# The last second layers of a perceiver kernel get tighter schedules, and the very last one stands alone behind the loop

## The chip, the cores and the metric

The kernel runs on one core of one Trainium2 chip. The metric is the device time of one execution in microseconds. Below, PE is TensorE (matmuls; PEld are its weight loads), DVE is VectorE, ACT is ScalarE, POOL is GpSimd and SP is SyncE, which issues the transfers.

## The reference

Input `x` has 32 batches of 64 rows of 256 numbers; `ctx_1024` has 32 batches of 1601 rows of 256 numbers. Six blocks are added to `x` one after the other:

```
x = x + xattn0(layernorm(x), ctx)     # a linear layer over x and the mean of ctx
x = x + attn0(layernorm(x))           # 16 heads over the 64 rows, with ALiBi slopes
x = x + ffn0(layernorm(x))            # shared experts, and 8 routed experts (top 2)
x = x + xattn1(layernorm(x), ctx)     # 16 heads: 64 queries against 1601 context rows
x = x + attn1(layernorm(x))           # recurrent block, below
x = x + ffn1(layernorm(x))            # two layers with ternary weights and 8-bit activations

attn1(x):  x = causal_conv(rmsnorm(x)) + x          # width 4 in time, then 256 x 256
           h, g = rmsnorm(x) by 4 heads -> 96 + 96   # a gated linear recurrence over 64 rows
           x = gru_out + x
           x = (silu(n @ w_gate) * (n @ w_value)) @ w_ff_out + x     # n = rmsnorm(x)
ffn1(x):   h = gelu(quant(x) @ ternary(w1).T);  out = quant(h) @ ternary(w2).T
```

## The kernel before

**Tiles and pieces.** The 32 batches are worked on in 16 tiles of two batches, 128 rows. A tile has a *position* 0 to 15 in the order of work; the last position holds tile 0. Almost all of the work is `xattn1`. It is a loop over 208 *pieces*, `g` = 0 to 207, 13 to a position: twelve pieces of 512 context rows for half the heads of one batch, and, as number 9 of each position, a *rest piece* with the last 65 context rows of both batches. The loop is written as a software pipeline with a fixed order on PE, DVE, ACT and POOL. In the turn of piece `g` it issues, in this order:

- `column_scores(g)`: the matmuls `s` (L842, L845, L851), and on ACT the two exponentials `pt` (L857), 1 us each
- `values(g + 4)`: the matmuls `vps` (L236), and on DVE the copy `vau` (L787)
- now and then a small transpose `tpm` (L826) for the row maxima
- **place 0**: steps of the other layers that begin with ACT work
- `row_scores(g + 5)`: the matmuls `r` (L803), and on DVE two maxima over them, `mx` (L810); after every third piece of a half also five small operations on the maxima (L816 to L821)
- place 0.5: steps that need the column form of matmuls
- `weighted(g)`: 64 matmuls `o` (L875), which need `pt` and `vau`
- `keys(g + 6)`: the matmuls `kps` (L248), and on ACT the copy `kt` (L770)
- **place 1**: all other steps

So towards the end of the loop the keys run out after the turn of piece 201, the row scores after that of 202 and the values after that of 203.

**Steps of the other layers.** Everything else (the first layers of later positions, the queries, the expert choice, the second layers) is written as Python generators. Each `yield` ends a *step*, and its value says to which place the next step belongs. An object of `Steps` lays the steps of one generator into the pieces: with `n` steps to do between the times `t0` and `t1` (given in sixteenths of a position and turned into pieces by `planned`), `run` does a step when `done * (t1 - t0) <= (now - t0) * n`. With `place` 3, at most one step is done in each place of a piece, and only if its kind belongs there.

**The second layer** of a position is `recurrent` and `bit_ffn` (L952 to L1133): 30 steps from `x4`, the result of `xattn1`, to the store of the output. What they do, with the names that the profile shows (K: in place 0, the others in place 1):

| steps | work |
|---|---|
| 1, 2 | statistics `st_e`, `mv_e`, `rstd_e` (POOL), `xn_e`, `yb` |
| 3 K, 4, 5 K | `xs_e` (squares on ACT, `rn_e` on POOL, product on DVE), transposes `tp_e`, ACT copies `ypad` |
| 6, 7 | the convolution `cT`: four DVE operations each (L970, L973) |
| 8 | matmuls `pw`, sum `y` |
| 9 K, 10 | `xs_f` |
| 11 K, 12 K | transposes `tp_f`, ACT copies `nT`; matmuls `hg`, four ACT tanh (`gg`, `zz`), DVE `rr` |
| 13, 14 | the gate chain (POOL `zz`; DVE `gg`, `gg`, `gg`, `zz`, a memset and the scan into `rr`, L1014 to L1022) |
| 15 | matmuls `gru`, sum `y`, POOL `xy` |
| 16 K, 17 | `xs_g` |
| 18 K, 19 K | `tp_g`, `nT`; first half of the matmuls `ff`, tanh `fth`, DVE `fm` (L257, L258) |
| 20, 21 K, 22 | `fm` (L260); second half of `ff`; `fm` (L260) |
| 23 | matmuls `ffo`, sum `x` (L1054), statistics `st_h`, `mv_h` |
| 24 | `xn_h`, its largest value `am_h`, scaled and rounded `qt`; POOL `q_h` |
| 25 K, 26 K | transposes `tpq_h`, ACT copy `qT_h`; matmuls `h` (L236) and ACT Gelu (L1124) |
| 27, 28 | `am_i`; two passes over `h` (L1070, L1071), POOL `q_i` |
| 29 K | transposes `tpq_i`, ACT copy `qT_i` |
| 30 | matmuls `h` (L244, L248), `x` (L1132), store to `out` by SP (L1133) |

`x4` of a position is made in the second piece of the next one (`projected`, `wo`). In the loop's place 1 the 128 x 128 matmuls are issued in four column parts (`mmq`, L248); outside it they are whole (L244). Position 15 uses a variant with two halves, `halved`, in place of steps 27 to 29. Tiles of a second layer have mostly one or two buffers per name, so two second layers share them in turn.

**Where the second layers lie before.** That of position p runs from piece 13(p + 1) + 2 over about 20 pieces, so two overlap for some pieces. Position 12: pieces 171 to 191. Position 13: 184 to 204. Position 14: it starts at 197, and 15 of its 30 steps are done when the loop ends. Behind the loop `projected` makes `x4` of position 15, and then the last lines

```
        while plan:
            for s in list(plan):
                s.step()
                ...
```

take one step of position 14 and one of position 15 in turn until both are done. This stretch is called the *tail*.

Of the kernel before, what the change touches and what calls it, by code (L numbers as in the profile page):

```python
# [21 lines left out]
NT = NB * S // P  # L22
# [22 lines left out]
def perceiver_kernel(ctx: ExitStack, tc: tile.TileContext, a: dict, out: bass.AP):  # L45
# [16 lines left out]
    ACT = "ACT"  # L62

    COL = "COL"
# [7 lines left out]
    def mm_tile(shape, name, dtype=F32):  # L72
        return ps_mm.tile(shape, dtype, tag="mm", name=name)
# [176 lines left out]
    def mmq2(o, lhsT, rhs):  # L250
        for c in range(2):
            mmq(o, lhsT(c), rhs(c), c == 0, c == 1)
# [559 lines left out]
    def maxima(h):  # L812

        hf = halves[h]
        ng = small.tile([P, 4], F32, tag="ng", name=f"ng_{hf.name}")
        nc.vector.tensor_reduce(ng, wholes[hf.pos].mx[:, :, h % 4, :], AX.X, ALU.max, negate=True)  # L816
        m = mxp[h % 2]
        nc.vector.tensor_copy(m[:, :, 0], ng)
        nc.vector.tensor_tensor(ng, ng, m[:, :, 0], ALU.subtract)
        nc.vector.tensor_copy(m[:, :, 1], ng)  # L820
        nc.vector.tensor_tensor(m[:, :, 2], ng, m[:, :, 1], ALU.subtract)  # L821

    def maxima_rows(h):
        hf = halves[h]
        t = mm_tile([P, P], f"tpm_{hf.name}", BF16)
        nc.tensor.transpose(t, mxp[h % 2].rearrange("p i c -> p (i c)"), identb)  # L826
        hf.neg = work.tile([P, P], BF16, tag="neg", name=f"neg_{hf.name}", bufs=5)
        nc.vector.tensor_copy(hf.neg, t)
# [113 lines left out]
    def projected(pos):  # L942

        w = wholes[pos]
        o = mm_tile([P, D], f"wo1_{w.ti}")
        mmq2(o, lambda c: w.oT[:, c].rearrange("p b s -> p (b s)"), lambda c: w_o2[:, c, :])
        x = work.tile([P, D], F32, tag="x4", name=f"x4_{w.ti}", bufs=1)
        nc.vector.tensor_tensor(x, o, residues[pos], ALU.add)
        return x
# [185 lines left out]
    def tail(ti, x):  # L1135
        x = yield from recurrent(ti, x)
        yield from bit_ffn(ti, x)
# [107 lines left out]
    class Steps:  # L1245
# [8 lines left out]
        def step(self):  # L1254
            if self.gen is not None:
                self.done += 1
                try:
                    self.kind = next(self.gen)
                except StopIteration:
                    self.gen = None  # L1260

        def run(self, t, place):
            at = place if self.place == 2 and place != 0.5 else self.place
            if self.place == 3:
                if {ACT: 0, COL: 0.5}.get(self.kind, 1) != place:
                    return
                at = place
            if at == place:
                now = t + (0.5 * place if self.place >= 2 else 0)
                while self.gen is not None and self.done * (self.t1 - self.t0) <= (now - self.t0) * self.n:  # L1270
                    self.step()
                    if self.place == 3:
                        break

        def all(self):
# [12 lines left out]
    def first_layer(pos, k=0):  # L1288
        x3[pos] = yield from layer0(order[pos], csums.get(pos), k)

    def queried(pos):
        yield from query(pos, x3[pos])

    def second_layer(pos):
        yield from tail(order[pos], x4[pos])
# [4 lines left out]
    def first():  # L1300

        csum = sums_tile(order[0])
        steps = layer0(order[0], csum, 0, True)
        for _ in range(3):
            next(steps)
            yield
        junk = big.tile([P, L], F32, tag="part", name="junk", bufs=2)
        summed(order[0], csum, 0, 0, ctxs[0][:, 0, :], junk)
        nc.vector.tensor_reduce(csum[:, 1, 0:1], ctxs[0][:, 1, :], AX.X, ALU.add)
        yield  # L1310
        next(steps)
        yield

        n = L // 2
        more = small.tile([P, 1], F32, tag="ss", name="more", bufs=4)
        summed(order[0], csum, 1, 0, ctxs[1][:, 0, :], junk)
        nc.scalar.activation(junk[:, :n], ctxs[1][:, 1, :n], AF.Copy, accum_out=more)
        nc.vector.tensor_reduce(csum[:, 1, 1:2], ctxs[1][:, 1, n:], AX.X, ALU.add)
        nc.vector.tensor_tensor(csum[:, 1, 1:2], csum[:, 1, 1:2], more, ALU.add)
        csums[0] = csum  # L1320
        yield
        x3[0] = yield from steps
        yield from query(0, x3[0])
# [7 lines left out]
    def early_sums():  # L1331
        for pos in range(1, 4):
            yield from sums(pos, 2)
# [3 lines left out]
    def planned(gen, t0, t1, n, place):  # L1337
        plan.append(Steps(gen, t0 * NU / 16, t1 * NU / 16, n, place))

    plan = []  # L1340
    planned(first_layer(2), 2, 15, 26, 2)
    for pos in range(1, NT):
        if pos > 2:
            t0 = 14 * (pos - 3) + 2 + 4 * (pos == 3)
            planned(first_layer(pos), t0, t0 + 27 - 4 * (pos == 3), 28, 3)
        if pos < NT - 1:
            planned(queried(pos), 16 * (pos - 1) + (1 if pos > 1 else 5), 16 * (pos - 1) + 8.5, 6, 0)
        planned(second_layer(pos - 1), 16 * pos + 1.5, 16 * pos + 31, 33, 3)
    for group, t0, t1 in ((range(4, 6), 5.5, 15), (range(6, 9), 16, 42), (range(9, 13), 45, 84), (range(13, 16), 88, 140)):
        planned(sums_of(group), t0, t1, 12 * len(group) + 2, 0)  # L1350
    for c, t0 in ((1, 72), (2, 128), (3, 184)):
# [7 lines left out]
    with tc.manual_schedule(engines={ET.PE, ET.DVE, ET.Activation, ET.Pool}):  # L1359
        ahead, beside, summing = Steps(first()), Steps(first_layer(1, 1)), Steps(early_sums())  # L1360

        def besides():
            if 1 in csums:
                beside.step()

        def scored():
            row_scores(scores.pop(0))

        scores = list(range(5))
        do = {"a": ahead.step, "b": besides, "s": summing.step, "r": scored, "w": late_weights, "m": lambda: maxima(0),  # L1370
              "t": lambda: maxima_rows(0)}
        do |= {f"k{g}": lambda g=g: keys(g) for g in range(6)} | {f"v{g}": lambda g=g: values(g) for g in range(3)}

        for what in """a a a a k1 a a k2 a a s s k3 k0 a a a a s s s s a k4 a v0 v1 a a a s s s s s s b a b a b a b a s w
                    a s s a a a b a a s s s r b r b s s s r k5 b r m s s s r v2 t""".split():
            do[what]()
        if beside.gen is not None:
            plan.insert(0, Steps(beside.gen, 0, 4, 28 - beside.done, 2))
        planned(biased(), 3, 5, 2, 1)
        if summing.gen is not None:  # L1380
            plan.insert(0, Steps(summing.gen, 0, 4.5, 37 - summing.done, 0))
        planned(all_ternary(), 5, 23, 24, 2)

        def run(t, place):
            for s in [s for s in plan if s.t0 <= t]:
                s.run(t, place)
                if t >= s.t1 and t < NU * NT - 1:
                    s.all()
                if s.gen is None:
                    plan.remove(s)  # L1390

        for g in range(NU * NT):
            pos, p = divmod(g, NU)
            if pos + 1 < NT:
                if p == 0:
                    wholes[pos + 1].rest = load_rest(order[pos + 1])
                if p in (2, 9):
                    load_batch(2 * pos + 2 + p // 8)
            column_scores(g)
            if g == 0:  # L1400
                values(3)
            if g + 4 < NU * NT:
                values(g + 4)
            if p == 1 and pos:
                normalise(pos - 1)
            if g == NU * NT - 2:
                normalise(pos, 3)
            if g + 4 < NU * NT and scanned(g + 4)[2] == NP - 1:
                maxima_rows(scanned(g + 4)[1])
            run(g, 0)  # L1410
            if g + 5 < NU * NT:
                row_scores(g + 5)
                if scanned(g + 5)[2] == NP - 1:
                    maxima(scanned(g + 5)[1])
            run(g, 0.5)
            weighted(g)
            if p == NU - 1 and pos < NT - 1:
                gathered(pos)
            if p == 3 * NP and pos == NT - 1:
                gathered(pos, 3)  # L1420
            if g == NU * NT - 5:
                picked()
            in_columns[0] = True
            if g + 6 < NU * NT:
                keys(g + 6)
            if p == 1 and pos:
                x4[pos - 1] = projected(pos - 1)
            run(g, 1)
            in_columns[0] = False
        normalise_last(NT - 1)  # L1430
        x4[NT - 1] = projected(NT - 1)
        plan.append(Steps(second_layer(NT - 1)))
        while plan:
            for s in list(plan):
                s.step()
                if s.gen is None:
                    plan.remove(s)
# [46 lines left out]
```

## Time and profile before

| | |
|---|---|
| median of three runs (lowest, highest) | 2059.86 us (2058.57, 2060.37) |
| the profiled execution, its own time | 2059.22 us |
| its span, first to last instruction | 2057.5 us |
| mean granted clock of TensorE | 0.982 |
| PE, DVE, ACT, POOL busy | 1960.1, 1300.4, 903.7, 324.8 us |
| the chain that ended last | PE 87%, DVE 7%, ACT 2% |
| `s` of pieces 201 to 207 starts in the chain of waits at | 1942.83, 1950.02, 1957.60 (its second half), 1963.13, 1970.33, 1975.13, 1979.43 us |
| last `o` ends, tail begins | 1983.73 us |

A row of the timeline gives the start in us from the span's beginning, the length in us, the engine, the line, the operation, output and inputs, the shapes and how many instructions were merged; in brackets stands the idle time of the engine before it and what ended it. The chain of waits is followed back from the last instruction and names at each time the work that everything after it waited for.

### The profile page before, as it was taken

The page shows a single profiled execution, that of the slowest core. Times are in us where ns is not written, and L with a number is a line of the kernel's source. Part 1 is how long each engine was busy: PE and PEld are TensorE (multiplying, and loading weights), DVE is VectorE, ACT ScalarE, POOL GpSimd, SP SyncE. Part 2 cuts the span into 40 slices and gives each one's busy share as a digit, 9 for nine tenths or more (in the row PEclk, how much of TensorE's full clock was granted, in tenths as well). Part 3 has the DMA queues.
Part 4 walks back from the last instruction along what each step waited for, and adds up shares of the span by engine and source line. Part 5 has one row for each costly group of instructions (what it writes and reads, how often), then busy time and mean ns, then how long its engine had stood idle before and what let it go on. Part 6 is the DMA issues. An engine that isn't in the chain of part 4 may idle for free.

```text
span 2057.5 us, 79682 instructions
## 1 busy us (share of the span) xinstructions
PE 1960.1 (95%) x36771; PEld 1367.5 (66%) x36771; DVE 1300.4 (63%) x2618; ACT 903.7 (44%) x1402; POOL 324.8 (16%) x543
## 2 busy tenths in 40 slices
PE   5889999999999999999999999999999999999975
PEld 3566677667676766676766676766766666666653
DVE  4556766666666765666667666666667766665654
ACT  4345454454545444444545434343443434334331
POOL 2121111111111111111111111111110111000011
PEclk9899999999999999999999999999999999999996
DMA  9225323221222212112120111111011211101000
GB/s 310 105 90 173 122 85 111 79 89 42 93 90 88 95 36 66 59 58 77 61 76 10 50 40 37 49 40 45 6 58 46 68 45 37 58 2 47 3 12 5
DMA packets 54806, 136.90 MB, mean 67 GB/s; under 512 B 13318, under 2 KB 35016, under 8 KB 54472
## 3 DMA queue, kind: packets, MB, share of 16 engines
q1 hardware_dynamic: 53912, 130.99, 18.8%
q8 instruction: 288, 4.72, 1.0%
q10 hardware_dynamic: 560, 0.81, 0.1%
q14 instruction: 46, 0.38, 0.1%
HBM read 125.53 MB, written 6.25 MB: 64 GB/s over the span
## 4 chain that ended last, share of the span: by engine, by line
PE 87%; DVE 7%; ACT 2%; issue 2%; DMA 1%; POOL 1%; SPq 0%; DVEq 0%; ACTq 0%; POOLq 0%
PE vps L236 18%; PE kps L248 15%; PE r L803 11%; PE o L875 9%; PE s L851 9%; PE ff L236 4%; PE s L845 3%; DVE mx L810 2%; PE ffo L248 2%; PE q L236 1%; ACT pt L857 1%; PE wo L248 1%; PE hg L1004 1%; PE k L236 1%; PE sv L236 1%
## 5 line engine op out<-in xcount | busy, mean ns | idle before, releaser
L857 ACT ACTIVATE pt<-s 128x1024 f32<-128x1024 f32 (+1 forms) x416 | 403.1, 1021 | 265.7 <-PE s L851 265.5
L810 DVE TENSOR_REDUCE mx<-r 128x2 f32<-128x1024 f32 x384 | 451.9, 1219 | 97.4 <-PE r L803 97.2
L236 PE MATMUL vps<-w_L_xattn_WvT,ctxT 128*128 128x128 f32 x3072 | 393.4, 281 | 0.0
L770 ACT ACTIVATE kt<-kps,chv 128x512 f32<-128x512 f32 x192 | 132.0, 687 | 584.9 <-PE kps L248 567.7
L236 PEld LDWEIGHTS vps<-w_L_xattn_WvT,ctxT 128*128 128x128 f32 x3072 | 357.4, 191 | 24.7 <-issue 3.4
L248 PE MATMUL kps<-ctxT,w_L_xattn_WkT 128*32 128x512 f32 x2992 | 356.7, 594 | 0.0
L787 DVE COPY vau<-vps 128x512 f32<-128x512 f32 (+1 forms) x208 | 143.5, 690 | 322.1 <-PE vps L236 320.8
L875 PEld LDWEIGHTS o<-pt,vau 128*32 128x32 f32 (+1 forms) x13312 | 197.7, 110 | 132.2 <-issue 118.5
L875 PE MATMUL o<-pt,vau 128*32 128x64 f32 (+1 forms) x13312 | 230.0, 221 | 5.2 <-ACT pt L857 5.0
L803 PE MATMUL r<-kt,qbd 32*128 32x512 f32 x1536 | 228.9, 647 | 2.8 <-DVE mx L810 2.0
L851 PE MATMUL s<-qbd,kt 32*128 32x128 f32 x6144 | 208.5, 271 | 0.0
L851 PEld LDWEIGHTS s<-qbd,kt 32*128 32x128 f32 x6144 | 205.9, 187 | 3.1
L248 PEld LDWEIGHTS kps<-ctxT,w_L_xattn_WkT 128*32 128x32 f32 x2992 | 83.6, 110 | 112.7 <-issue 112.7
L803 PEld LDWEIGHTS r<-kt,qbd 32*128 32x128 f32 x1536 | 65.9, 184 | 41.0 <-issue 21.2
L845 PEld LDWEIGHTS <-onesb 3*128 3x128 bf16 x768 | 21.3, 91 | 104.2 <-issue 102.1
L845 PE MATMUL s<-neg,onesb 3*128 3x512 bf16 x768 | 82.7, 385 | 5.9 <-DVE mx L810 4.9
L294 ACT ACTIVATE part<-part 128x1601 f32<-128x1601 f32 x48 | 74.1, 1544 | 0.0
L236 PE MATMUL ff<-nT,w_fg 128*128 128x128 f32 x384 | 51.7, 287 | 1.0 <-ACT nT L1039 1.0
L370 POOL TENSOR_TENSOR kbd<-kT,mask 128x512 f32<-128x512 f32 x32 | 32.6, 1040 | 114.9 <-ACT kT L363 114.9
L236 PE MATMUL ff<-nT,w_fv 128*128 128x128 f32 x384 | 50.4, 283 | 0.0
L236 PEld LDWEIGHTS ff<-nT,w_fg 128*128 128x128 f32 x384 | 47.8, 200 | 1.9 <-ACT nT L1039 1.8
L236 PEld LDWEIGHTS ff<-nT,w_fv 128*128 128x128 f32 x384 | 47.9, 201 | 0.0
(384 smaller groups left out, 2376.9 us busy)
## 6 DMA issues: line engine op xcount, KB each, us to landing
ctxT<-ctxT SPq DMA_DIRECT2D x31, 1601.0 KB
part<-ctxT SPq DMA_DIRECT2D x60, 800.5 KB
od<-osb SPq DMA_DIRECT2D x15, 256.0 KB
rest<-ctxT SPq DMA_DIRECT2D x32, 65.0 KB
x<-x SPq DMA_DIRECT2D x16, 128.0 KB
out<-x SPq DMA_DIRECT2D x16, 128.0 KB
w<-w SPq DMA_DIRECT2D x16, 128.0 KB
rs<-od SPq DMA_DIRECT2D x30, 64.0 KB
```

What stands on the lines that cost most here:

```text
L236: nc.tensor.matmul(o, lhsT=lhsT(c), rhs=rhs(c), start=(c == 0), stop=(c == 1))
L248: nc.tensor.matmul(o[r], lhsT=lhsT[:, r], rhs=rhs, start=start, stop=stop)
L294: nc.scalar.activation(parts[j], parts[j], AF.Copy, accum_out=csum[:, c, 2 * i + b:2 * i + b + 1])
L370: nc.gpsimd.tensor_tensor(kbd[oc], kT[:, oc, :].rearrange("p (b k) -> p b k", b=2).unsqueeze(2).to_broadcast([P, 2, 4, S]), mask4.unsqueez ...
L770: nc.scalar.activation(kt, o, AF.Identity, bias=chv[:, hf.oc, BK2:BK2 + 1])
L787: nc.vector.tensor_copy(v[:kr, :, 0:VW - 16].rearrange("p k (h d) -> p k h d", d=17)[:, :, :, 0:16], o[:kr].rearrange("p k (h d) -> p k h ...
L803: nc.tensor.matmul(o, lhsT=qbd[r, q % 2, q // 2].rearrange("p h q -> p (h q)"), rhs=w.kt[r, q, :] if h is None else halves[h].kt[k][r, :], ...
L810: nc.vector.tensor_reduce(w.mx[:, 2 * m:2 * m + 2, h % 4, k], ps[m], AX.X, ALU.max)
L845: nc.tensor.matmul(o, lhsT=onesb[r, :], rhs=halves[h].neg[r, :].unsqueeze(1).to_broadcast([3, 4, P]), start=True, stop=False)
L851: nc.tensor.matmul(ps[i // 2][:kr, i % 2, j * P:(j + 1) * P], lhsT=w.kt[r, j, :] if h is None else halves[h].kt[k][r, j * P:(j + 1) * P], ...
L857: nc.scalar.activation(pt[:kr].rearrange("p i k c -> p i (k c)"), ps[m][:kr], AF.Exp)
L875: nc.tensor.matmul(w.o[32 * c:32 * c + 32, q, m, :], lhsT=v[:kr, j, 17 * hd:17 * hd + 32], rhs=pts[m][:kr, c // 2, j, c % 2 * S:c % 2 * S ...
```

## The change

Three things are changed. The end times of the plans for the second layers of positions 12, 13 and 14 (entries NT - 3, NT - 2 and NT - 1) are earlier: 16 pos + 28, + 18 and + 15 in place of + 31. Positions 13 and 14 get the new `place` 4: several steps are done in one place, as long as the schedule is behind and the next step's kind belongs to that place. Behind the loop all that is left of other plans is finished before position 15's second layer is put into the plan.

Laid out by the formula of `run`, position 12 has its steps in the same pieces as before. Position 13 has them in pieces 184 to 195: among others steps 6, 7, 8 in piece 186 (place 1), 11, 12 in 188 (place 0), 13, 14 in 188, 18, 19 in 191 (place 0), 22, 23 in 192, 25, 26 in 194 (place 0) and 27, 28 in 194. Position 14 has them in pieces 197 to 206: steps 6, 7, 8 in 199, 11, 12 in 201 (place 0), 13, 14, 15 in 201, 18, 19 in 203 (place 0), 22, 23, 24 in 204, 25, 26 in 205 (place 0), 27, 28 in 205, 29 and 30 in 206.

```diff
@@ class Steps
+        def fits(self, place):
+            return {ACT: 0, COL: 0.5}.get(self.kind, 1) == place
+
         def run(self, t, place):
             at = place if self.place == 2 and place != 0.5 else self.place
-            if self.place == 3:
-                if {ACT: 0, COL: 0.5}.get(self.kind, 1) != place:
+            if self.place >= 3:
+                if not self.fits(place):
                     return
                 at = place
             if at == place:
                 now = t + (0.5 * place if self.place >= 2 else 0)
                 while self.gen is not None and self.done * (self.t1 - self.t0) <= (now - self.t0) * self.n:
                     self.step()
-                    if self.place == 3:
+                    if self.place == 3 or self.place == 4 and not self.fits(place):
                         break
@@ the plans
-        planned(second_layer(pos - 1), 16 * pos + 1.5, 16 * pos + 31, 33, 3)
+        t0, t1 = 16 * pos + 1.5, {NT - 3: 16 * pos + 28, NT - 2: 16 * pos + 18, NT - 1: 16 * pos + 15}.get(pos, 16 * pos + 31)
+        planned(second_layer(pos - 1), t0, t1, 33, 3 if pos < NT - 2 else 4)
@@ behind the loop
         x4[NT - 1] = projected(NT - 1)
+        for s in plan:
+            s.all()
         plan.append(Steps(second_layer(NT - 1)))
```

## The prediction

> **What bounds the kernel now.** I read the page first, then the chain of waits over the last 200 us, then the stretches of time around the loop's end, then the timeline row by row.
>
> ```profile
> PE 1960.1 (95%) x36771; PEld 1367.5 (66%) x36771; DVE 1300.4 (63%) x2618; ACT 903.7 (44%) x1402; POOL 324.8 (16%) x543
> PEclk9899999999999999999999999999999999999996
> ```
>
> TensorE is busy 95% of the span and at full clock until the last slice. The table by stretches (us, busy of PE, PEld, DVE, ACT, POOL, then granted clock, DMA share, GB/s) shows where that ends:
>
> ```profile
> 1890.00:1942.00 52.00, 52.00 (x990) 36.13 (x986) 28.11 (x48) 18.79 (x28) 4.64 (x10) 1.00 0.04 12
> 1956.00:1984.00 28.00, 20.50 (x650) 16.54 (x639) 14.52 (x33) 13.99 (x20) 4.73 (x10) 0.94 0.07 22
> 2000.00:2024.00 24.00, 11.98 (x60) 8.15 (x59) 15.52 (x38) 6.25 (x13) 4.57 (x8) 0.68 0.01 5
> 2024.00:2057.00 33.00, 16.64 (x84) 12.49 (x84) 12.38 (x32) 4.45 (x10) 3.49 (x7) 0.66 0.02 5
> ```
>
> Until 1942 us TensorE has no free time: whatever is put there, or makes it wait there, lengthens the run one for one. From piece 202 on (`s` at 1950.02; keys, row scores and values run out) it has gaps. After 1984 us there is only the tail: 73.3 us of second layers, a chain of small steps.
>
> **The tail loses 14.1 us.** Before, steps 16 to 30 of position 14 are laid between the steps of position 15. Timeline rows of the tail (start, length):
>
> ```profile
> 1990.71 0.57 POOL L212 TENSOR_TENSOR rn_e<-rn_e,mhalf 128x1 f32<-128x1 f32 x1
> 1995.12 0.56 DVE L258 TENSOR_TENSOR fm<-fm,ff 128x384 f32<-128x384 f32 x1 [1.42 <-PE ff L236]
> 1995.59 0.35 DVE L214 TENSOR_SCALAR xs_e<-xn_e,rn_e 128x256 f32<-128x256 f32 x1
> 2004.26 0.39 DVE L979 TENSOR_TENSOR y<-pw,yb 128x256 f32<-128x256 f32 x1
> 2011.80 2.03 PE L1004 MATMUL hg<-nT,w_hg 64*96 64x128 f32 x16 [0.61 <-ACT nT L987]
> 2023.91 0.42 DVE L1029 TENSOR_TENSOR y<-gru,y 128x256 f32<-128x256 f32 x1 [1.11 <-PE gru L244]
> ```
>
> Position 15's `xs_e` has its input at 1991.3 and waits behind position 14's `fm` until 1995.59: 4.2 us. From `xs_e` to `y` 8.67 us passed; alone it is 0.39 + transposes at half clock 0.70 + first `ypad` 0.38 + eight `cT` operations 3.03 + the last two `pw` matmuls 0.80 = 5.3, so 3.35 less. From `y` to `hg` 7.54; alone 0.43 and then 3.23 (the same steps for `xs_g` took 3.38 from 2024.43 to 2027.81, 0.15 of it behind `xy`): 3.85 less. From `hg` to the next `y` 12.11; alone 3.71 to the end of `rr` (2015.51), 3.7 for the gate chain on VectorE, 1.9 for `gru`: 2.8 less. Together 14.2. What follows 2023.91 is alone already; there the Gelu table load (1.28 us at 2008.84, now done by position 14 in the loop) comes back, beside the `h` matmuls, for 0.15. Net 14.1.
>
> **Work moved into the full part costs 4.8 us.** By the formula in `run`, and by the changed program's order of instructions, position 12 keeps its pieces; position 13 ends at piece 195 instead of 204; position 14 has 15 steps done by piece 201 instead of 7 and ends at piece 206. Ahead of piece 202 TensorE so gets steps 26 to 30 of position 13 (`h` 0.86, `tpq_i` 0.45, `h` 0.87) and 8 to 15 of position 14 (`pw` 0.86, as the equal `wo` of 1905.14, `tp_f` 0.23, `hg` 1.05, `gru` 0.45). The rows of SP, POOL and ACT that move (output store, memsets, `rstd`) have engines that are under half busy.
>
> **New waits: three long, 11.0 us.** Steps that stood a piece apart now follow each other in one place, and a matmul that waits for VectorE holds up the next piece, as `r` stood behind the waiting `tpo` at 1718 us (below). VectorE's rows in the loop:
>
> ```profile
> 1875.80 0.41 DVE L1014 TENSOR_SCALAR gg<-gg 96x512 f32<-96x512 f32 x1
> ...
> 1884.91 1.22 DVE L1022 TENSOR_TENSOR_SCAN rr<-zz,gg 96x512 f32<-96x512 f32 x1
> ...
> 1930.15 2.36 DVE L810 TENSOR_REDUCE mx<-r 128x2 f32<-128x1024 f32 x2 [0.38 <-PE r L803]
> ...
> 1933.37 0.18 DVE L821 TENSOR_TENSOR mxp<-ng,mxp 128x4 bf16<-128x4 f32 x1
> 1935.68 0.42 DVE L1054 TENSOR_TENSOR x<-ffo,xy 128x256 f32<-128x256 f32 x1 [2.14 <-PE ffo L248]
> ```
>
> - Piece 199, steps 6 to 8 of position 14: `mx` and the five maxima operations hold VectorE until 0.52 after the keys (1933.55 against 1933.03); then `cT` 3.03, then the last four `pw` matmuls 0.55: 4.1, less `pw` itself 0.86: 3.25.
> - Piece 186, the same steps of position 13: position 12's `ffo` covers the maxima, but its `x` and statistics stand ahead of `cT` on VectorE, 1.17 after `ffo` ends; 1.17 + 3.03 + 0.55 - 0.86 = 3.9.
> - Piece 201, steps 13 to 15 of position 14: the gate chain starts as in 1875.80, level with the end of the keys (1875.75), and is 0.41 + 0.69 + 0.68 + 0.42 + 0.07 + 1.22 and gaps, 3.75; `gru` waits for all of it: 3.8.
>
> Four shorter ones add 2.6: `hg`, `ff` and `h` now wait for ACT's copy made in the same place, behind the two `pt` (pieces 188, 194 and 201: about 0.45 each, the wait of `ff` for `nT` at 2027.81 being 0.5; piece 191, behind the 1.01 us `qT_i` copy as well: 1.2).
>
> **The clock: 4.8 us.** Gaps in TensorE's work cost clock afterwards. In the timeline of a stall at 1718 us:
>
> ```profile
> 1718.72 0.69 PE L644 MATMUL tpo<-ident,ohw 128*128 128x128 f32 x2 [1.46 <-POOL ohw L638]
> 1719.34 2.09 PE L803 MATMUL r<-kt,qbd 32*128 32x512 f32 x8
> 1721.36 1.45 PE L875 MATMUL o<-pt,vau 128*32 128x64 f32 x64
> ```
>
> `r` takes 1.14 and `o` 1.10 elsewhere, `tpo` 0.44; the clock row shows 0.50 from 1720 to 1722. That is 1.55 us; gaps of 0.42 and 0.48 at 525 us cost 1.7 (`kps` 3.39 for 1.90). The equal short gaps at 1854 us cost nothing. I take 1.6 for each of the three long waits, none for the short ones; ends 0 and 9.6 (two such stints each). The Trainium skill, "TensorE: Matmul & The Clock Gate", section "HAM oscillation — how this bites in real kernels", speaks of idle gaps over about 3.4 us; both rows above had shorter ones and lost the clock, and by the rule only the wait at piece 201 would count (the other two are broken by `pw`'s first half), which would make the sum 3.2 us smaller.
>
> **The last six pieces: 9.7 us more.** Before, from `s` of piece 202 (1950.02) to the last `o` (1983.73) 33.7 us pass. After, counted from that `s`: 1.22 + values 1.9 + `r` 1.07 + `o` 1.03; `s` of 203 waits for `mx` and ends at 8.0 (as at 1958.8); values 9.9; `tp_g`, a wait for `nT` 10.75; `ff` 2.73, `o`, `s`, `ff` 2.73, `o` of the rest piece 1.3 and `ffo` 2.6 bring it to 22.5. Then steps 23 to 30, which took six pieces and now take three, hold TensorE. In the chain of waits:
>
> ```profile
> 1965.37 1.05 POOL q_i L1074
> ...
> 1966.47 0.62 PE tpq_i L1079 x8
> ...
> 2043.50 0.41 PE tpq_h L1079 x2
> 2044.36 1.90 PE h L236 x4
> ```
>
> `tpq_h` comes 4.9 after `ffo` ends (tail: 2038.58 to 2043.50), Gelu ends 3.5 later (2043.50 to 2046.98; the table load fits behind the copy), `tpq_i` 4.7 after Gelu (2013.38 less 2011.52, both passes over `h`, POOL's 1.05 and gaps), then 0.62, `o` 1.1, `h` 1.0, `s` 1.25 and 3.1 to the last `o`: 20.2. That is 42.7, and 44.4 with half clock after both gaps; 43.4 taken, 33.7 off.
>
> **Sum.** The profiled execution took 2059.22 us (span 2057.5), 0.6 below the median of the runs; 2059.2 + 4.8 + 11.0 + 2.6 + 4.8 + 9.7 - 14.1 = 2078.0. A measurement of this kernel can tell about 0.2%, 4 us, from no change.
>
> **Rivals.**
> - The waits are covered (faster). If VectorE finished each chain while TensorE still works off what stands ahead, at pieces 186, 199, 201, 205 and 206, the long and short waits, their clock and some 8 us of the last pieces would go: 2078.0 - 11.0 - 2.6 - 4.8 - 7.8 = 2051.8. It decides for faster when waits, clock and last pieces together (28.1) fall under 14.1 - 4.8 = 9.3. For it: VectorE is only 54% busy from 1890 to 1942. Against: its order is fixed, and the rows show it with `mx` until the keys end. 0.11.
> - The clock holds: no stint at half speed, last pieces at 8.8: 2072.3. For it: gaps at 1854. 0.22.
> - Two stints after each long wait and half clock throughout the last pieces: 2078.0 + 4.8 + 2 = 2085. 0.10.
> - Waits about half as long, balancing the tail, within 4 us of before: 0.05.
> - That position 14 still reaches the tail: the changed order of instructions has its last matmul ahead of `s` of piece 207, so no chance is given.
>
> **How the numbers follow.** The forecast has 0.52; 2078 is its sum. Slower by over 0.2%: 0.52 + 0.22 + 0.10 = 0.84; within 0.05; faster 0.11. The range, 2062 to 2088: below, no clock loss, the waits 4 us shorter and the last pieces at 6 give 2065, with 3 towards the balanced case; above, the worst clock and 3 us more of waiting.
>
> **What would show it.** Right: TensorE waiting about 3 to 4 us before `pw` (twice) and `gru` for VectorE, then `s`, values at half clock; waits of 3 to 5 us before `tpq_h` and `tpq_i` in the last pieces; the tail from the last `o` to the end near 59 us. Wrong: `pw` and `gru` starting within 1 us of the keys, or a tail still over 65 us.

## The result, and the profile after

The changed kernel takes 2086.32 us (median of four runs, 2082.53 to 2088.39) against 2060.11 us (four runs of the kernel before, 2058.57 to 2060.54). The ratio is 1.0126, 95% interval 1.0111 to 1.0142: 26.2 us slower, where 18.8 was forecast; 2086.3 lies inside the range, close to its upper end. The profiled execution after took 2088.39 us, the longest of the four (span 2086.7). The account below is made against it, and so has to explain 29.2 us of span, 3 more than the medians differ.

The page's rows of busy time and granted clock after:

```profile
PE 1971.1 (94%) x36815; PEld 1373.9 (66%) x36831; DVE 1300.6 (62%) x2618; ACT 905.7 (43%) x1404; POOL 324.8 (16%) x543
PEclk9899999999999999999999999999999999999875
```

TensorE is 11 us longer at work although no work was added (some of position 14's matmuls are only cut into column parts, since they now stand in the loop): its clock falls in the last three slices, where before it fell only in the last. (The 8 in the second slice is in both kernels.) The chip does the same work in another order, so the times are best compared by stage. Here are four marks in each trace: the keys `kps` issued in the turn of piece 186, `s` of piece 202, the end of the last `o`, and the end (starts and ends from the timelines).

| us | pieces 186 to 201 | pieces 202 to 207 | tail | span |
|---|---|---|---|---|
| before | 126.12 | 33.78 | 73.77 | 2057.5 |
| after | 152.47 | 48.24 | 61.27 | 2086.7 |
| difference | +26.35 | +14.46 | -12.50 | +29.2 |

The remaining 0.87 lies ahead of piece 186; 0.65 of it is already there at 1786 us, where the two kernels still do the same. The tail does get shorter; more is paid ahead of it. For the first stage, this is the table by stretches of before (first line; it ends 0.07 us later than the mark) and after (second), with the columns stretch, length, busy time of PE (instructions), PEld, DVE, ACT, POOL, then granted clock, DMA share and GB/s:

```profile
1823.83:1950.02 126.19, 125.29 (x2472) 84.73 (x2464) 77.78 (x149) 50.70 (x73) 9.98 (x20) 1.00 0.06 21
```

```profile
1824.70:1977.17 152.47, 138.07 (x2576) 92.28 (x2567) 87.34 (x168) 57.69 (x85) 13.02 (x25) 0.95 0.05 18
```

Half of the loss is TensorE standing still (0.9 us before, 14.4 after: +13.5), and half is TensorE at work for longer (+12.8: moved work, and work at a lower clock). Who is waited for, in the view of PE's waits after, same stretch (us in total, times, longest):

```profile
PE pw L248 <- DVE cT L973: 5.9, 4, 3.2
PE gru L248 <- DVE rr L1022: 3.9, 1, 3.9
PE ff L236 <- ACT nT L1039: 1.1, 1, 1.1
PE tpq_i L1079 <- POOL q_i L1074: 1.1, 1, 1.1
PE hg L1004 <- ACT nT L987: 1.0, 2, 0.5
PE r L803 <- ACT pt L857: 0.8, 2, 0.5
PE h L236 <- ACT qT_h L1081: 0.5, 1, 0.5
```

Before, only the line of `r` is there, with 0.9. The first of the long waits, in the timeline after:

```profile
1829.26 0.42 DVE L1054 TENSOR_TENSOR x<-ffo,xy 128x256 f32<-128x256 f32 x1 [1.97 <-PE ffo L248]
...
1830.28 0.31 DVE L970 TENSOR_SCALAR cT<-ypad,chv 128x128 f32<-128x128 f32 x1
...
1830.63 1.62 DVE L973 SCALAR_TENSOR_TENSOR cT<-ypad,chv,cT 128x128 f32<-128x128 f32 x3
...
1832.39 1.08 PE L248 MATMUL pw<-w_pw,cT 128*32 128x256 f32 x8 [3.20 <-DVE cT L973]
...
1833.71 1.08 PE L248 MATMUL pw<-w_pw,cT 128*32 128x256 f32 x8 [0.24 <-DVE cT L973]
...
1834.72 0.61 PE L845 MATMUL s<-neg,onesb 3*128 3x512 bf16 x4
...
1835.12 1.92 PE L851 MATMUL s<-qbd,kt 32*128 32x128 f32 x32
```

VectorE does position 12's `x` and statistics first, then the eight `cT` operations, and `pw` waits for them with the next piece's `s` behind it. Both halves of `pw` then take 1.08 each (0.86 had been assumed for the two together), and `s` takes 1.92 for about 1.1: the clock has fallen too. The table by stretches after shows how far and for how long:

```profile
1828.89:1832.31 3.42, 0.30 (x8) 0.00 (x0) 2.88 (x8) 0.00 (x0) 1.56 (x3) 1.00 0.00 0
1832.31:1835.72 3.41, 3.09 (x32) 1.35 (x36) 1.67 (x5) 0.00 (x0) 0.00 (x0) 0.50 0.00 0
1835.72:1839.13 3.41, 3.41 (x38) 3.19 (x31) 0.00 (x0) 1.98 (x3) 0.00 (x0) 0.50 0.00 0
1839.13:1842.54 3.41, 3.41 (x89) 2.17 (x91) 2.22 (x4) 0.35 (x2) 0.80 (x2) 1.00 0.02 5
1952.00:1958.50 6.50, 6.25 (x62) 4.25 (x62) 1.49 (x5) 1.84 (x3) 0.00 (x0) 0.50 0.01 3
1976.00:1982.00 6.00, 5.85 (x80) 5.40 (x81) 0.43 (x2) 2.33 (x4) 0.73 (x1) 0.50 0.01 3
```

The clock is 0.50 from 1832.31 to 1839.13, and equally long, 6.8 us, from 1951.77 and from 1975.66: after each of the three long waits.

### The profile page after: what moved, and what is told of

It is laid out like the page before. It is cut to its first block, busy times and chain, and to the rows that moved or that the text cites. A ratio compares the mean times of both kernels' runs of the same rounds, so it can differ in the third digit from the quotient of the medians.

```text
span 2086.7 us, 79792 instructions
## 1 busy us (share of the span) xinstructions
PE 1971.1 (94%) x36815; PEld 1373.9 (66%) x36831; DVE 1300.6 (62%) x2618; ACT 905.7 (43%) x1404; POOL 324.8 (16%) x543
## 4 chain that ended last, share of the span: by engine, by line
PE 86%; DVE 8%; ACT 3%; issue 2%; POOL 1%; DMA 0%; SPq 0%; DVEq 0%; ACTq 0%; POOLq 0%
PE vps L236 18%; PE kps L248 14%; PE r L803 11%; PE o L875 9%; PE s L851 9%; PE ff L236 4%; PE s L845 3%; DVE mx L810 3%; PE ffo L248 2%; PE q L236 1%; ACT pt L857 1%; PE wo L248 1%; PE hg L1004 1%; PE k L236 1%; PE sv L236 1%
## 5 line engine op out<-in xcount | busy, mean ns | idle before, releaser
L236 PEld LDWEIGHTS vps<-w_L_xattn_WvT,ctxT 128*128 128x128 f32 x3072 | 358.8, 192 | 25.1 <-issue 3.9
L845 PEld LDWEIGHTS <-onesb 3*128 3x128 bf16 x768 | 21.5, 91 | 104.4 <-issue 102.5
L845 PE MATMUL s<-neg,onesb 3*128 3x512 bf16 x768 | 83.6, 389 | 6.7 <-DVE mx L810 5.7
L257 DVE TENSOR_SCALAR fm<-ff 128x384 f32<-128x384 f32 x32 | 17.9, 558 | 46.5 <-ACT fth L256 46.5
```

Of the source, the lines that this page charges most:

```text
L236: nc.tensor.matmul(o, lhsT=lhsT(c), rhs=rhs(c), start=(c == 0), stop=(c == 1))
L845: nc.tensor.matmul(o, lhsT=onesb[r, :], rhs=halves[h].neg[r, :].unsqueeze(1).to_broadcast([3, 4, P]), start=True, stop=False)
```

## The experiments

The theory: several steps of one second layer in one place make TensorE wait for VectorE inside the full part of the loop, and the waits also cost clock. Its rivals: the long way through the last pieces alone is what costs, or the loop's clock falls for another reason, or one of the three edits alone carries all of it. In the diffs the surrounding code is that of the changed kernel or of the kernel before, as said.

**Waits filled with unused matmuls (`fill`)**, the changed kernel with:

```diff
+    def fill(ti, name, n):
+        if n:
+            o = mm_tile([P, 512], f"fill_{name}_{ti}")
+            for _ in range(n):
+                nc.tensor.matmul(o, lhsT=w_k2[:, 0, 0:P], rhs=w_fg[:, 0, 0:512], start=True, stop=True)
...
+        fill(ti, "pw", {order[NT - 3]: 3, order[NT - 2]: 2}.get(ti, 0))
...
+        fill(ti, "gru", {order[NT - 2]: 4}.get(ti, 0))
```

> The changed kernel with matmuls into an unused PSUM tile put on TensorE ahead of the three waiting matmuls: three ahead of pw of position 13 (gap 3.2 us), two ahead of pw of position 14, four ahead of gru of position 14 (gap 3.9 us), 0.86 us each. The waits stay as long as they are; only TensorE is busy in them. If the half clock after a wait is a cost of its own: s and vps of pieces 187, 200 and 202 return from 2.3 and 2.9 to 3.4 us to 1.2 and 2.0, pw and gru from 1.08 to 0.9 and 0.45: about 2.2 + 2.2 + 3.1 = 7.5 us less than the changed kernel, 2079. If the half clock costs nothing on the path, or the added matmuls stand in the way: 2086 or more.

Measured: 2079.95 us (2075.50 to 2084.58), ratio 1.0093 (1.0070 to 1.0117). More work on TensorE makes the run 6.4 us faster than the changed kernel by the medians; the two intervals just overlap, so the reading rests on the stages of the traces. The table by stretches of `fill`, around the same three places:

```profile
1831.00:1835.00 4.00, 3.57 (x26) 1.32 (x21) 3.00 (x8) 0.00 (x0) 1.56 (x3) 1.00 0.00 0
1835.00:1841.50 6.50, 5.81 (x91) 3.86 (x95) 2.67 (x8) 2.33 (x4) 0.75 (x2) 1.00 0.00 0
...
1954.50:1961.00 6.50, 6.50 (x137) 4.27 (x129) 3.54 (x6) 2.33 (x4) 1.31 (x3) 1.00 0.01 3
1973.00:1979.00 6.00, 5.73 (x95) 3.98 (x93) 2.10 (x3) 2.33 (x4) 1.11 (x3) 1.00 0.01 3
```

The clock stays at 1.00. Pieces 186 to 201 take 147.45 (5.0 less than after) and the last pieces 46.17 (2.1 less), the tail 61.31 as after. So the half clock behind the three waits costs about 7 us, and the chains on VectorE remain: the first half of `pw` of piece 186 starts at 1834.96 here and at 1832.39 in the changed kernel, just the 2.57 us apart that the two traces already are at the keys of that turn. The second half now waits 0.69 for VectorE, at pieces 186 and 199 alike, where it waited 0.24 and 0.25 behind the slower first half: not all that TensorE gains reaches the run.

**Steps apart again (`apart`)**, the changed kernel with one more place to stop, after steps 7 and 14, so that `pw` and `gru` come a piece after `cT` and the gate chain:

```diff
-                    if self.place == 3 or self.place == 4 and not self.fits(place):
+                    if self.place == 3 or self.place == 4 and (self.done in (7, 14) or not self.fits(place)):
```

> The changed kernel, but no place goes on past step 7 or step 14, so pw and gru of positions 13 and 14 come a piece later than their VectorE chain. If the long waits and the half clock after them are the main cost: the waits of 4.7, 3.7 and 4.6 us and the slow s and vps after them go, about 17 us; position 14 slips by a piece, two of its steps run behind the loop ahead of position 15, 3 to 5 us: 2072 to 2075. If the work moved into the full part of the loop is the main cost: within 4 us of the changed kernel, 2083 to 2087.

Measured: 2079.57 us (2075.23 to 2083.07), ratio 1.0090 (1.0070 to 1.0111): half of what was expected. By stages the theory holds: the waits at `pw` and `gru` are gone, no stretch at half clock is left in these pieces (the next begins at 1974.7, among the last pieces, where before has one at 1967.9), and pieces 186 to 201 take 136.91, 15.6 less than after. Of the 10.8 that are left over before, 4.4 are TensorE's longer work and 6.4 are waits, two of which are longer than after: the view of PE's waits of `apart` in this stretch begins

```profile
PE hg L1004 <- ACT nT L987: 2.0, 1, 2.0
PE tpq_h L1079 <- DVE vau L787: 1.7, 1, 1.7
PE tpq_i L1079 <- POOL q_i L1074: 1.1, 1, 1.1
```

And with two more stops position 14's last two steps no longer fit into the loop. In the timeline of the tail:

```profile
2015.52 1.06 PE L1079 MATMUL tpq_i<-identb,q_i 128*128 128x128 bf16 x8
2017.68 1.89 PE L244 MATMUL h<-wq_L_ffn_w2T,qT_i 128*128 128x256 bf16 x8 [1.10 <-ACT qT_i L1081]
2024.25 0.69 PE L220 MATMUL tp_e<-ident,xs_e 128*128 128x128 f32 x2 [4.68 <-DVE xs_e L214]
```

They stand ahead of position 15's first `tp_e`, and the tail is 67.33, 6.1 longer than after. The last pieces take 46.22, and what lies ahead of piece 186 is 2.3 longer: -15.6 - 2.0 + 6.1 + 2.3 is the difference of the spans, -9.2. Most of the expected gain was made in the loop, and six of it given back in the tail.

**Position 13 alone (`only13`)**, the kernel before with `place` 4 and the new end time for position 13 only:

```diff
-        planned(second_layer(pos - 1), 16 * pos + 1.5, 16 * pos + 31, 33, 3)
+        t0, t1 = 16 * pos + 1.5, {NT - 2: 16 * pos + 18}.get(pos, 16 * pos + 31)
+        planned(second_layer(pos - 1), t0, t1, 33, 4 if pos == NT - 2 else 3)
```

> The kernel before with position 13 alone on the changed plan (end 16 pos + 18, place 4); position 14, and the tail with both layers in turn, as before. By the waits: 4.7 + 2.2 us at piece 186, short waits 3.7 us (pieces 188, 191, 194, 195), 2.2 us of work moved ahead of piece 202, less about 5 us that pieces 202 to 204 lose of position 13's steps 26 to 30 and two table loads: 2060 + 8 = 2068. If all the loss comes from position 14: 2060.

Measured: 2071.53 us (2070.81 to 2071.62), ratio 1.0052 (1.0037 to 1.0067): 11.3 us slower. Pieces 186 to 201 take 139.27 (+13.15), the last pieces 32.03 (-1.75; position 13 ends ahead of them), the tail 73.5 as before. Half of the loss in pieces 186 to 201 belongs to an edit that does not touch the tail at all.

**Position 14 alone (`only14`)**, the changed kernel with position 13 on its old plan; position 14 gets buffers of its own for `h`, `x6` and the tiles that share their names, since the two positions now overlap in another order (that part is not shown):

```diff
-        t0, t1 = 16 * pos + 1.5, {NT - 3: 16 * pos + 28, NT - 2: 16 * pos + 18, NT - 1: 16 * pos + 15}.get(pos, 16 * pos + 31)
-        planned(second_layer(pos - 1), t0, t1, 33, 3 if pos < NT - 2 else 4)
+        t0, t1 = 16 * pos + 1.5, {NT - 1: 16 * pos + 15}.get(pos, 16 * pos + 31)
+        planned(second_layer(pos - 1), t0, t1, 33, 3 if pos < NT - 1 else 4)
```

> The changed kernel with position 13 back on the plan of before (it ends at piece 204); position 14 on the changed plan, with buffers of its own for the names that the two layers would otherwise share in the wrong order. By the waits: 10.6 us of waits and clock and 2.2 us of moved work of position 13 go, and position 13's steps 26 to 30 come back into pieces 202 to 204, which are full of position 14's steps, 5 us: 2086 - 12.8 + 5 = 2078. If position 13 costs nothing: 2086 or, with its steps back in the last pieces, 2091.

Measured: 2077.77 us (2076.73 to 2079.04), ratio 1.0085 (1.0067 to 1.0103): 17.5 us slower. Pieces 186 to 201 take 139.85 (+13.73), the last pieces 50.80, the tail 60.73. In the loop the two edits simply add up: 13.15 + 13.73 = 26.9 against 26.35 with both. Together the two runs give 28.8, close to the 26.2 of the whole change.

**The tail's own order (`serialtail` and `tailorder`).** What had the tail before paid for position 14's steps 16 to 30, which the change moves ahead? `serialtail` is the kernel before with the third edit alone:

```diff
         x4[NT - 1] = projected(NT - 1)
+        for s in plan:
+            s.all()
         plan.append(Steps(second_layer(NT - 1)))
```

> The kernel before, with the third part of the change alone: behind the loop position 14's remaining 15 steps are all finished before position 15's second layer begins; the plans in the loop are the old ones. Theory (laying the two second layers between each other hides most of position 14's half, so that the tail of before costs only 12 to 14 us over position 15 alone): position 15 alone takes the 61.25 us measured in the changed kernel, and the 15 steps of position 14 alone some 32 us (in the tail of before, position 15 took 33.6 from the y of its step 15 to the end, the store included); 61.3 + 32 is 93 against 73.8, so 19 us slower, about 2079. Rival (position 14's steps hardly overlap with anything before either, the two only share their gaps): 2065 or less.

Measured: 2078.12 us (2072.81 to 2081.30), ratio 1.0084 (1.0064 to 1.0104); the tail is 90.50.

`tailorder` is the kernel before with the loop at the end replaced by an order written out by hand, and with buffers of its own for position 15:

```diff
-        while plan:
-            for s in list(plan):
-                s.step()
-                if s.gen is None:
-                    plan.remove(s)
+        left, last = plan[0], Steps(second_layer(NT - 1))
+        for what in """p l p l p l l l l l p l p l l p l p l l l p l l p l l p l p l p p l l l p l p""".split():
+            (left if what == "p" else last).step()
+        left.all()
+        last.all()
```

> The kernel before with its loop unchanged; only the order behind it is different: the 15 remaining steps of position 14 and the 30 of position 15 are laid by hand, so that position 14's matmuls go out while position 15's chain is on VectorE, ScalarE or GpSimd, and position 15 no longer stands behind position 14's VectorE work (xs_e had waited 4.2 us, xs_e to y lost 3.35, y to hg 3.85, hg to the next y 2.8). Position 15 also gets its own buffers for h and x6. Theory (what the tail loses is a matter of order: VectorE's and TensorE's fixed order puts position 14's steps ahead of position 15's chain at the wrong moments): the tail falls from 73.8 to 64 to 66 us, the run from 2060 to about 2051. Rival (the volume of position 14's work on the engines is what costs, whatever its order): the tail stays at 72 to 75 and the run within 3 us of 2060.

Measured: 2050.70 us (2043.47 to 2056.23, seven runs), ratio 0.9956 (0.9938 to 0.9973): faster than both kernels. The tail is 62.68. Four rows of its timeline show why: position 15's `xs_e` starts right behind its `rn_e` (before: 4.2 us later, behind `fm`), and position 14's `ff` fills TensorE while `cT` is on VectorE.

```profile
1989.98 0.57 POOL L212 TENSOR_TENSOR rn_e<-rn_e,mhalf 128x1 f32<-128x1 f32 x1
1990.58 0.35 DVE L214 TENSOR_SCALAR xs_e<-xn_e,rn_e 128x256 f32<-128x256 f32 x1 [1.80 <-POOL rn_e L212]
...
1990.99 0.69 PE L220 MATMUL tp_e<-ident,xs_e 128*128 128x128 f32 x2 [2.58 <-DVE xs_e L214]
...
1991.47 2.71 PE L236 MATMUL ff<-nT,w_fg 128*128 128x128 f32 x12
```

With position 15 alone in the tail at 61.27, the same 15 steps of position 14 so cost 29.2 us in series (90.50), 12.5 taken in turn (73.77), and 1.4 when each matmul stands where position 15 waits (62.68). Which part of the last step the order makes and which the buffers, these runs do not separate.

**More of the clock (`fillall` and `warmtail`).** `fillall` is `fill` with unused matmuls ahead of position 14's `tpq_h` and `tpq_i` as well:

```diff
+        fill(name, "tpq", {f"h{order[NT - 2]}": 3, f"i{order[NT - 2]}": 1}.get(name, 0))
         t = mm_tile([P, 8, P], f"tpq_{name}", BF16)
```

> The changed kernel with unused matmuls ahead of pw and gru, as in the kernel fill, and 3 and 1 more ahead of tpq_h and tpq_i of position 14 in pieces 205 and 206; the results are not used. Theory (the last pieces were mis-sized because half clock follows the two waits of 3.74 and 1.34 us there: o 1.94 for 1.10, s 1.79 for 1.06, o of piece 206 1.72 for 0.99, h 1.88 for 1.0): these go back to full clock and the run falls by 2 to 3 us under fill's 2080, to 2077 to 2078, the forecast. Rival (the last pieces are set by ScalarE and VectorE, and TensorE's clock there does not matter): 2080 again.

Measured: 2079.24 us (2074.14 to 2085.27), ratio 1.0102 (1.0084 to 1.0119), not to be told from `fill`. `o` and `s` of pieces 205 and 206 did go back to full clock (`o` 1.10, `s` 1.06), but `tpq_i` started at 2010.34 against 2010.44 in `fill`: it is set by the chain from `h` through Gelu and VectorE to `q_i`, so the time saved on TensorE became a longer wait (2.78 for 1.34), which cost the clock behind it again (0.50 from 2009.43 to 2016.26). The last pieces take 45.15 for 46.17 in `fill`, and the tail 62.02 for 61.31. So for that stretch the rival was right in the main.

`warmtail` is `tailorder` with short unused matmuls (128 columns) ahead of the waiting matmuls of the tail; those ahead of `tpq_i` of position 15 (14) and of the last `h` of position 14 (3) are not shown:

```diff
+        fill(f"tp_{name}", {f"g{NT - 1}": 5, "e0": 8, "g0": 10}.get(name, 0))
...
+        fill(f"gru_{ti}", {0: 9}.get(ti, 0))
...
+        fill(f"tpq_{name}", {"h0": 7}.get(name, 0))
```

> The kernel tailorder with short unused matmuls (128 columns) ahead of tp_g of position 14, of tp_e, gru, tp_g, tpq_h and tpq_i of position 15 and of the last matmuls of position 14, about as long at full clock as the waits seen there; the results are not used. Theory (the tail's matmuls run at half clock because of its gaps, and some 17 us of them stand on its chain): with the clock held 3 to 6 us go, the run at 2045 to 2048 against 2050.7. Rival (the clock does not come back in so broken a stretch, and at half clock the unused matmuls take twice their time and stand in the way): 2052 to 2056.

Measured: 2048.64 us (2043.51 to 2051.23), ratio 0.9954 (0.9940 to 0.9968). In the profiled execution the clock is 1.00 all through the tail, and the tail is 57.76 for 62.68:

```profile
1984.04:2041.80 57.76, 42.72 (x356) 36.75 (x345) 33.88 (x85) 13.74 (x33) 11.50 (x23) 1.00 0.02 6
```

```profile
1983.02:2045.70 62.68, 36.53 (x244) 28.82 (x233) 34.07 (x85) 13.73 (x33) 11.50 (x23) 0.75 0.02 5
```

(The first line is `warmtail`, the second `tailorder`.) That is a gain of 4.9 us in the trace, but 1.7 of it goes in pieces 186 to 201 of the same execution, which was the fastest of its six (2043.51, the others 2047.69 to 2051.23), and the ratios of the two kernels cannot be told apart. The theory holds for the clock; for the time it stays unproved.

## Why the prediction was right, and where its sizes were off

The sign and the mechanism were right, and the sum was 10.4 us short of the profiled execution. The account against the profiled execution, in us:

| step of the sum | predicted | measured |
|---|---|---|
| work moved ahead of piece 202 | +4.8 | +6.3, what the other rows leave |
| three long waits | +11.0 | 3.44 + 2.48 + 3.90 = +9.8 |
| four short waits | +2.6 | 0.51 + 1.15 + 0.47 + 0.46 = +2.6 |
| a wait of `tpq_i` in piece 195 | 0 | +1.1 |
| half clock in pieces 186 to 201 | +3.2 | about +6.5, of which `fill` won 5.0 |
| last six pieces, with the half clock after piece 201 | +11.3 | +14.5 |
| tail | -14.1 | -12.5 |
| ahead of piece 186 | 0 | +0.9 |
| sum | +18.8 | +29.2 |

**Moved work.** The matmuls that came into pieces 186 to 201 were priced at 4.8. In `fill`, at full clock, their groups take 6.2 us more than before. A part of the difference is `pw`: issued in two halves with a wait between, each half takes 0.64, where 0.86 had been assumed for both together.

**Waits.** Piece 186 was said to wait 3.9 and waited 3.20 and 0.24, piece 199 3.25 and waited 2.23 and 0.25, piece 201 3.8 and waited 3.90. Counted as the prediction did, at full clock and less `pw` or `gru` itself, `fill` shows 4.3, 3.3 and 4.1 from the keys to the next `s`: 11.7 for 11.0. `apart` shows that they are what it costs to have these steps in one place. One wait was not foreseen: in piece 195, `tpq_i` stands for 1.11 us behind POOL's `q_i`, the same dependence that the prediction had priced in the last pieces only.

**The clock is the term that was most mis-sized.** It was put at one stretch of 3.4 us at half clock, 1.6 us, for each long wait, from the stall at 1718 us; its upper bound had two. It was two each time. The groups of instructions by shape, before and then after, in the stretch from the keys of 186 to `s` of 202 (xcount, busy us, mean ns of one, idle before):

```profile
L851 PE MATMUL s<-qbd,kt 32*128 32x128 f32 x448 | 15.3, 271 | 0.0
...
L236 PE MATMUL vps<-w_L_xattn_WvT,rest 128*65 128x128 f32 x32 | 3.9, 276 | 0.0
...
L248 PE MATMUL pw<-w_pw,cT 128*32 128x256 f32 x16 | 1.0, 378 | 0.0
```

```profile
L851 PE MATMUL s<-qbd,kt 32*128 32x128 f32 x448 | 17.1, 291 | 0.0
...
L236 PE MATMUL vps<-w_L_xattn_WvT,rest 128*65 128x128 f32 x32 | 6.0, 363 | 0.0
...
L248 PE MATMUL pw<-w_pw,cT 128*32 128x256 f32 x32 | 4.3, 632 | 5.9 <-DVE cT L973 5.9
```

The same 448 and 32 matmuls take 1.8 and 2.1 us more, and each half of `pw` 1.08 for 0.64 in `fill`, 1.8 in all. With the small part of `s` (L845, 0.61 for 0.40, twice) and `gru` (1.08 for 0.65) this is about 6.5. `fill` shows what of it was the clock's price to the run: 5.0 in these pieces, where 3.2 was predicted, and 2.1 behind piece 201, together 7.1 for the 4.8 of the sum. The rest of the 6.5 did not reach the run, above all because the second half of `pw` then waits for VectorE instead. The single row that the price came from was a fair example but not the rule.

The Trainium skill's page "TensorE: Matmul & The Clock Gate" (section "HAM oscillation — how this bites in real kernels") gives idle gaps of over about 3.4 us as what takes the clock away. The waits of 3.20 and 0.24 and of 2.23 and 0.25 us are singly under that and lost 6.8 us of full clock just like the one of 3.90; the measurement decides against reading the rule as a limit. Its figure of 3413 ns for the window (same page, "Part 1: The HAM clock gate (the "warmup" mystery)") does agree with the stretches seen: 3.4 us at 1718, twice that here.

Why two here and one there? In each of the ten traces the clock record changes only on one grid of 3.41 us. Around the stall at 1718 us of before, cut along its grid:

```profile
1715.33:1718.74 3.41, 1.41 (x15) 0.93 (x13) 2.08 (x6) 0.70 (x2) 1.24 (x2) 1.00 0.00 0
1718.74:1722.15 3.41, 3.41 (x42) 1.58 (x46) 0.69 (x1) 0.37 (x1) 0.00 (x0) 0.50 0.00 0
```

There the wait ends with its window; the next window, at half clock, has TensorE busy throughout, and the clock is back after it. At piece 186 (the lines in the section on the profile after) the wait reaches into the first window at half clock, where TensorE is busy 3.09 of 3.41 us, and the clock comes back only after a second one that is full. Pieces 199 and 201 are alike (3.05 and 2.93). In `tailorder`, whose loop is that of before, the very stall at 1718 us cost no clock at all: the same 1.46 us fall on the grid so that more of TensorE's work shares their window, and `r` behind it takes 1.14 for 2.09.

```profile
1719.57 0.44 PE L644 MATMUL tpo<-ident,ohw 128*128 128x128 f32 x2 [1.46 <-POOL ohw L638]
```

```profile
1717.53:1720.94 3.41, 1.95 (x17) 0.85 (x16) 0.77 (x2) 0.37 (x1) 1.24 (x2) 1.00 0.00 0
1720.94:1724.35 3.41, 3.41 (x90) 1.86 (x88) 3.17 (x5) 0.46 (x1) 0.00 (x0) 1.00 0.02 5
```

So where a wait falls on the grid goes with whether it costs none, one or two windows, and one row could not give its price. The exact condition stays open: at 2016.62 of the changed kernel's trace one window with 2.90 us of work was enough to bring the clock back, less than the 2.93 to 3.09 that were not.

**The last six pieces.** The way to the end of position 14's `ffo` was put at 22.5 after `s` of 202 and took 25.1; in `fill` it took 22.6. So the 2.5 us are the third stretch at half clock, and the chain was worked out rightly. From there 20.2 was predicted, 20.9 with the clock, and 23.1 measured. `tpq_h` (4.96 after `ffo`, 4.9 predicted) and `tpq_i` (8.07 later, 8.2 predicted) were right. Of the waits of 3 to 5 us named as signs, that of `tpq_h` was 3.74, but that of `tpq_i` only 1.60: `o` and `s` ahead of it ran at half clock and filled the time. The rest is in the timeline after:

```profile
2013.85 1.28 ACT L857 ACT_TABLE_LOAD   x1 [3.09 <-PE s L851]
...
2015.36 0.62 PE L1079 MATMUL tpq_i<-identb,q_i 128*128 128x128 bf16 x8 [1.60 <-POOL q_i L1074]
...
2016.22 0.32 PE L875 MATMUL o<-pt,vau 128*32 128x64 f32 x8 [0.24 <-ACT pt L857]
...
2017.14 1.72 PE L875 MATMUL o<-pt,vau 128*32 128x64 f32 x56 [0.60 <-ACT pt L857]
...
2018.63 1.74 PE L248 MATMUL h<-wq_L_ffn_w2T,qT_i 128*32 128x256 bf16 x32
```

After Gelu ScalarE loads the table for the exponentials again, 1.28 us, and starts that only when `s` is done (3.09 idle). So `pt` is late, and `o` of piece 206 waits 0.24 and 0.60 for it, where `o` 1.1 without a wait had been assumed; then `o` (1.72 for 0.99, twice) and `h` (1.74 for 1.0) run at half clock. That is 0.8 and 2.2 us, together about the 2.9 over 20.2. `fillall` warns against calling all of the second part TensorE's: without half clock ahead of it, the chain through ScalarE, VectorE and POOL holds `tpq_i` at the same moment.

**The tail.** The predicted gain of 14.1 became 12.5. Up to the end of `wo` it lost what was thought untouched: from the last `o` to there 3.13 before and 4.51 after, since `picked` takes 1.97 for 1.10 and `wo` follows at half clock. Why the clock falls so early there, from 2023.45, the runs leave open: the waits just ahead of it, `o` for `pt` with 1.18 and 0.60 at 2022.77 and 2023.69, stand in the kernel before too (at 1981.83 and 1982.74), where the clock held until 1988.39. The parts worked out for position 15 alone were each a little short: from `xs_e` to `y` 5.84 for 5.3, from `y` to `hg` 3.92 for 3.66, from `hg` to the next `y` 9.72 for 9.3, together 1.2. From `y` behind `gru` (2053.74) to the end it took 32.9, before 33.6.

**The rivals.** The measured time is nearest to the rival of two stretches after each long wait, with half clock through the last pieces (2085), and in part for the reason that it gave: there were two stretches after each wait, but they cost 7.1 by `fill` where it had 9.6. That it came so near is luck as well, since the moved work, `tpq_i`, the last pieces and the tail were each short in it too. The rival for a gain, that VectorE finishes each chain under cover, needed waits, clock and last pieces under 9.3 us; they were 34.5 by the table above (9.8 + 2.6 + 1.1 + 6.5 + 14.5), and some 3 less if the medians are taken.

## What to carry to other kernels

In this kernel, `pw` and `gru` cost no wait as long as a piece of other work lay between them and their VectorE chain (before and `apart`), and a full wait, plus the clock behind it, when they stood in one place of the TensorE-bound loop. A wait of 2 to 4 us there cost itself plus about 2.3 us (`fill`: 7 us for three). A tail that two chains share is first to be put in the right order: the same 15 steps cost 29, 12.5 or 1.4 us there, and about 41 when they were pressed into the end of the loop together with those of position 13 (26.35 + 14.46).

## What the runs showed of the hardware

- Unused matmuls in a waiting TensorE can make a kernel faster: 6.4 us here by the medians; in the traces the stages behind the three waits are 7.1 us shorter, at a clock of 1.00 for 0.50.
- In `warmtail` single waits of up to 1.99 us (`ffo` for `fm`), with work on both sides, left the granted clock at 1.00; in the changed kernel 2.23 + 0.25 us lost it.
- The clock record changes on one grid of 3.41 us in every trace here, so a wait's place on that grid, and not only its length, can set its price.
- Some VectorE operations took about twice their time while POOL worked. In the timeline after, `xs_f` beside POOL's memset, and `xs_g` with POOL idle:

```profile
2042.13 0.70 DVE L214 TENSOR_SCALAR xs_f<-y,rn_f 128x256 f32<-128x256 f32 x1 [1.60 <-POOL rn_f L212]
2042.15 0.52 POOL L997 MEMSET rr<- 32x512 f32 x1
...
2056.03 0.35 DVE L214 TENSOR_SCALAR xs_g<-y,rn_g 128x256 f32<-128x256 f32 x1 [1.86 <-POOL rn_g L212]
```

  In the wait at piece 186 it is on the path: the three `cT` operations at 1830.63 take 1.62, the last of them 0.84 beside POOL's `xb` (1831.38, 0.72), and the three at 1832.53 take 1.12, 0.35 each. The Trainium skill's page "SBUF — State Buffer" (section "Who interferes with whom") tells of a port that VectorE and GpSimd share; the rows fit that, and no run here takes POOL's work away to show it.
